# A scan kernel on one core: decays kept in the states' tiles, stores issued an iteration later, one broadcast load in place of two, and an iteration's room for image work by its feed

## The chip, the cores and the metric

The kernel runs on one core of a Trainium2 chip. The metric is the device time in microseconds (us) of one execution; the time before is the median of three runs.

## The reference

The input `x` is [8, 64, 64, 96] in float32: eight images, 64 by 64 positions, 96 channels. Layer 0 adds to it a two-dimensional selective scan:

```
xz = groupnorm(x) @ in_proj_w.T                 # 96 -> 2 x 192, halves xh and z
xc = silu(depthwise 3x3 conv of xh + conv_b)
xs = xc along 4 paths: diagonals, antidiagonals, and both reversed     # 4096 steps each
dt, B, C = x_proj_weight of xs                  # 6, 16 and 16 values per step and path
delta = softplus(dt projected to 192 + bias)
for each of 4096 steps, 192 channels, 16 states n:
    h[n] = h[n] * exp(delta * A[n]) + delta * u * B[n]
    y = sum over n of h[n] * C[n]
y = y + D * xs, the 4 paths put back and added
x = x + (layernorm(y) * silu(z)) @ out_proj_w.T
```

Layer 1 works on each image's 4,096 tokens: a layer norm, six attention heads without softmax, `(q k^T) v`, which the kernel takes in the other order, so that a small Gram matrix per image is enough, then a layer norm and a two-layer perceptron whose factors are rounded to an 8-bit float. Both are added to the tokens.

## The kernel before

**The scan loop.** All work is held together by one loop in `run`. A *step* `m` is an image, a direction `q` (forward or backward) and a chunk of T = 512 of the 4,096 path positions: 8 x 2 x 8 = 128 steps. Both paths of a direction are done together: 2 paths x 64 channels fill 128 partitions, and G = 3 groups of 64 channels make 192. A step has 16 *iterations*, one for each state `n`, so the loop has 2,048 iterations `i = 16 m + n`. The recording order is the order of each engine's instructions: the file schedules by hand, and each engine executes its own queue in order. The framework adds the semaphore waits.

One iteration works on several states at once:

- `decay(i + 2)` on ACT (L966): three exponentials of 128 x 512, the factors `exp(delta * A[n])`, into a `decay` tile, of which there are three.
- `times_b(i + 2)`: the fed value `delta * u * B[n]`, turned, into a `feedT` tile. Who does it is read from `FEED = "DADADAGADADAAAAA"`, a letter for each state: A is ACT (L988, eight instructions of 128 x 192), G is GpSimd (L979), and for D nothing is done here.
- `recur(i)` on VectorE: three scans (L1009), one for each group, from the decays and the PSUM tiles `feed0` to `feed2` into an `h` tile, of which there are six. For a D state VectorE first makes the feed itself, by three multiplications in PSUM (L1013).
- For each part 0, 1 and 2 on TensorE: `turn(i + 1, part)`, which puts the next state's feed of that group into PSUM (four transposes, L996, or for a D state one product with `pick`, L998, in part 0), and then `reduce(i - 4, part)`, four transposes of an older `h` that add up the 16 states in PSUM (L1044).
- `keep(i - 1)` and `read(i - 1)` on GpSimd: the carry for the next chunk (L1025) and `h * C[n]` over 128 x 1536 in place (L1030).
- `fetch(i + 4)`: C[n] of the step as a row of 512 values, broadcast from DRAM (`crow`) to 64 partitions for each of the two paths, into a `cc` tile of [128, 512], of which there are five. It is two loads on SP's queue (L957), one for each path.

After state 15 `place` copies the summed `y` out of PSUM; the forward direction stores it (`part`, L1072), the backward one adds both and stores it, spread to the image (`spread`, L1080 and L1089).

**The images' work.** What comes before and after the scans for each image runs beside the loop, in pieces: `prologue(m)` (the projections of step m, with `crow`'s store at L910 and `delta`), `front` (norm, convolution, `gate`, and `walk`, which reads the image along its diagonals by loads `ut`, L587), and `tail` (`join` and `layers`, with stores of `mid`, `turned` and `out`). These are generators. Each says by a `yield` which engine it needs next and for about how long: `act(us)`, `dve(us)`, `gp(us)`, `pe(us)`, `bank(us)` (TensorE with a PSUM bank). The class `Work` resumes them at fixed places of an iteration, `work.at(tag, place)`: "A" between `decay` and `times_b`, "V" before the third scan, "P" after each part, "G" after `read`, and "S" at the start of an iteration. Each place has a credit: it grows by a gain for each visit, up to a most, and work is resumed while it is positive. `PLACES` holds gain and most. `LAGS` says how many iterations a piece waits after its last engine.

DMA is issued by SP (`nc.sync`) alone, in order: when an issue waits for a semaphore, all that follow wait.

Of the kernel before, what the change touches and what calls it, by code (L numbers as in the profile page):

```python
# [9 lines left out]
F32 = mybir.dt.float32  # L10
# [3 lines left out]
ALU = mybir.AluOpType  # L14
# [21 lines left out]
G = 3  # L36
# [218 lines left out]
    return "P", us, lag, "long" if long else "short"  # L255


SPIN = ("P", 0.0, -1, False)


class Work:
# [1 line left out]

    PLACES = {"A": (2.0, 2.5), "V": (1.5, 2.0), "G": (3.5, 5.0), "P": (0.85, 1.2), "S": (9.0, 9.0)}

    def __init__(self, banks):
        self.now = 0
# [44 lines left out]

        self.long = [x for x in self.long if x is not b]

    def at(self, tag, place=0):
        gain, most = self.PLACES[tag]
        self.credit[tag] = min(most, self.credit[tag] + gain)
        for j in self.urgent + ([] if self.hurried else self.jobs):  # L320
            while not j.done and j.tag == tag:
                if j.ready > (self.now, place) and (j.spin or not self.alone):
                    break
                if not self.alone:
                    if self.credit[tag] <= (0.0 if j not in self.urgent else -1.5 if tag == "P" else -99.0):
# [40 lines left out]
    def finish(self, enough):  # L366

        self.alone = True
        while not enough():
            self.next()  # L370
            for tag, place in (("A", 0), ("V", 0), ("P", 2), ("G", 0)):
                self.at(tag, place)
        self.alone = False
        self.credit = dict.fromkeys(self.PLACES, 0.0)

    def hurry(self, enough):

        self.alone = self.hurried = True
        while not enough():
            self.now += 1  # L380
            for tag, place in (("A", 0), ("V", 0), ("P", 2), ("G", 0)):
                self.at(tag, place)
        self.alone = self.hurried = False

# [89 lines left out]
def front(tc, work, x, k, at, b):  # L474
# [8 lines left out]
    with tc.tile_pool(name=f"f1_{b}", bufs=1, **area) as p1, tc.tile_pool(name=f"f2_{b}", bufs=2, **area) as p2:  # L483
# [33 lines left out]
        def convolve(c):  # L517
# [40 lines left out]
            nc.scalar.activation(pre[:, 0 : len(tiles), :], pre[:, 0 : len(tiles), :], AF.Silu)  # L558
            nc.scalar.activation(z, z, AF.Silu)
            k.tables()  # L560
            nc.sync.dma_start(out=at.gate[:, :, c * CH : (c + 1) * CH], in_=z)

            image = at.image[0 : HH * DOUBLE].rearrange("(h a x c) -> h x a c", a=2, c=DI, x=WW)
# [12 lines left out]
    with tc.tile_pool(name=f"f3_{b}", bufs=3, **area) as p2:  # L576

        def walk(c):
            ut = p2.tile([P, TB, G, 2, GC], F32, tag="ut", name="ut")
            for d in range(2):  # L580
                stride = (2 * WW + 1) * DI if d == 0 else (2 * WW - 1) * DI
                for v in range(2):
                    first = (c * (T // HH) + v + d * WW) * DI
                    rows = at.image[first : first + HH * stride].rearrange("(h x) -> h x", x=stride)
                    rows = rows[:, 0 : TB * 2 * DI].rearrange("h (k x) -> h k x", k=TB)[:, :, 0:DI]
                    for g in range(G):
                        nc.sync.dma_start(  # L587
                            out=ut[v * HH : (v + 1) * HH, :, g, d, :], in_=rows[:, :, g * GC : (g + 1) * GC]
                        )
            u = p2.tile([P, G, T], F32, tag="us", name="us")  # L590
            for g in range(G):
                ps = yield bank(0.45, 4 if g == 0 else 0)
                for i in range(TB):
                    nc.tensor.transpose(ps[:, i * P : (i + 1) * P], ut[:, i, g].rearrange("p d i -> p (d i)"), k.ident)
                yield act(0.6)
                nc.scalar.copy(u[:, g, :], ps)
                work.release(ps)
            for d in range(2):
                nc.sync.dma_start(
                    out=at.seq[d][:, c * T : (c + 1) * T].rearrange("(g i) t -> i g t", i=GC),  # L600
                    in_=u[d * GC : (d + 1) * GC],
                )
            at.walked.add(c)

        yield [walk(c) for c in range(NST)], 3


def tail(tc, work, x, out, k, at, b, last=False):
# [4 lines left out]
    with tc.tile_pool(name=f"t1_{b}", bufs=1, **area) as p1:  # L613
# [5 lines left out]
        with tc.tile_pool(name=f"t2_{b}", bufs=8 if last else 2, **area) as p2:  # L619
# [3 lines left out]
            def join(c):  # L623
# [61 lines left out]
                        )  # L685
                yield act(0.5)
                nc.scalar.copy(t, po)
                if not last:
                    nc.sync.dma_start(out=at.mid[:, s, :], in_=t)
                work.release(ps)  # L690
                yield dve(1.7)
                for i in range(4):
# [32 lines left out]
                if last:  # L725
                    kept[c] = t, xaT
                else:
                    nc.sync.dma_start(out=at.turned[:, c * CH : (c + 1) * CH], in_=xaT)
                joined.add(c)

# [31 lines left out]
        with tc.tile_pool(name=f"t3_{b}", bufs=8 if last else 3, **area) as p2:  # L762

            def layers(c):
# [66 lines left out]
                yield gp(2.0)  # L831
                nc.gpsimd.tensor_tensor(y16, y16, k.b2q, ALU.add)
                nc.gpsimd.tensor_tensor(t, t, y16, ALU.add)
                nc.sync.dma_start(out=out[b].rearrange("(t p) c -> p t c", p=P)[:, s, :], in_=t)

            yield [layers(c) for c in range(NCH)], 8 if last else 3
# [2 lines left out]
def run(tc, psum, dram, x, out, w, NB):  # L839
# [31 lines left out]
            )  # L871
        return images[b]

    made, decays, feeds, hs, carry, sums, other = {}, {}, {}, {}, {}, {}, {}
# [4 lines left out]
    def prologue(m):  # L879
# [26 lines left out]
        x = o.x = tile("x", [NX, T])  # L906
        nc.scalar.activation(x, v, AF.Identity, bias=w.xb)  # L907
        work.release(ps)
        o.crow = dram.tile([2 * NS, T], F32, tag="crow", name=f"crow_{m}", bufs=3)
        nc.sync.dma_start(out=o.crow, in_=x[XC:NX, :])  # L910


        delta = tile("delta", [P, G, T])
        for g in range(G):
            ps = yield bank(0.85)
            nc.tensor.matmul(ps, w.ws[:, q, g, :], x[0 : 2 * NR + 1, :], start=True, stop=True)  # L916
            yield dve(0.6)
            nc.vector.tensor_copy(delta[:, g, :], ps)  # L918
            work.release(ps)
# [32 lines left out]
    def fetch(i):  # L952

        m, n = divmod(i, NS)
        cc = made[m].c[n] = pool.tile([P, T], F32, tag="cc", name=f"cc_{i}", bufs=5)
        for d in range(2):
            nc.sync.dma_start(  # L957
                out=cc[d * GC : (d + 1) * GC], in_=made[m].crow[d * NS + n : d * NS + n + 1, :].to_broadcast([GC, T])
            )

    def decay(i):
        m, n = divmod(i, NS)
        _, q, _ = steps[m]
        decays[i] = pool.tile([P, G, T], F32, tag="decay", name=f"decay_{i}", bufs=3)
        for g in range(G):
            nc.scalar.activation(decays[i][:, g, :], made[m].delta[:, g, :], AF.Exp, scale=w.a_neg[:, q, g, n : n + 1])  # L966

    def times_b(i):

# [30 lines left out]
    def recur(i):  # L1000
        m, n = divmod(i, NS)
        _, q, _ = steps[m]
        h = hs[i] = pool.tile([P, G, T], F32, tag="h", name=f"h_{i}", bufs=6)
        a = decays.pop(i)
        back = slice(None, None, -1) if q else slice(None)

        def scan(g):
            init = carry[m - 1][:, n, g : g + 1] if m % NST else 0.0
            nc.vector.tensor_tensor_scan(h[:, g, back], a[:, g, back], feed[g][:, back], init, ALU.mult, ALU.add)  # L1009

        if FEED[n] == "D":
            for g in (1, 2, 0):
                nc.vector.tensor_tensor(feed[g], feed[0], made[m].du[:, g, :], ALU.mult)  # L1013
# [44 lines left out]
    def place(m):  # L1058
# [7 lines left out]
        for d in range(2):  # L1066
# [1 line left out]
                rows[:, d].rearrange("p k (g i) -> p k g i", i=GC),  # L1068
                y.rearrange("p (k g) (d i) -> p d k g i", g=G, d=2)[:, d],
            )  # L1070
        if q == 0:
            nc.sync.dma_start(out=image(b).part[:, c, :], in_=ys)  # L1072
        else:
            work.start(spread(m, rows), urgent=True)

    def spread(m, rows):
        b, q, c = steps[m]
        for d in range(2):
            yield gp(1.8, 1)
            nc.gpsimd.tensor_tensor(  # L1080
                rows[:, d], rows[:, d], other[m].rearrange("p (d k c) -> p d k c", d=2, k=TB)[:, d], ALU.add
            )
            stride = (3 * WW + 1) * DI if d == 0 else (3 * WW - 1) * DI
            for v in range(2):
                for again in range(2):
# [56 lines left out]
        work.now += tag == "A"  # L1142
        work.at(tag, at)

    LAG = 4
    for i in range(4):
        fetch(i)
    for i in range(2):
        decay(i)
        times_b(i)  # L1150
    for g in range(G):
# [3 lines left out]
    for i in range(total + LAG + 1):  # L1155
# [124 lines left out]
```

## Time and profile before

| | |
|---|---|
| median of 3 runs | 11,243.42 us (11,231.5 to 11,244.23) |
| the profiled execution | 11,245.66 us, of it 11,243.9 us span |
| mean granted TensorE clock | 0.907 |
| scan loop, first scan to last | 244 to 10,996 us |
| busy: TensorE, VectorE, ACT, GpSimd | 81%, 84%, 84%, 83% of the span |
| HBM traffic | 875 MB read, 320 MB written, 106 GB/s |

The profile's span runs from the first instruction to the last of one execution. A group of instructions is a line of the program with its operation and tiles; for it the profile gives busy time, mean duration, and the idle time of the engine just before, with what ended it. Engines are PE (TensorE's products), PEld (its weight loads), DVE (VectorE), ACT, POOL (GpSimd) and SP, whose queue entries are written SPq. A view of waits has, for each pair of waiter and releaser, microseconds in total, times and the longest. A view of windows has, for each stretch, its length, each engine's busy time with its number of instructions, then the TensorE clock, the share of the 16 DMA engines that was busy, and GB/s.

### The profile page before, as it was taken

How to read it: one execution, taken by the hardware profiler on the slowest of the kernel's cores; microseconds unless marked ns; L12 is line 12 of the kernel's file. 1: busy time of each engine (PE TensorE's matmuls, PEld its weight loads, DVE VectorE, ACT ScalarE, POOL GpSimd, SP SyncE). 2: the span in 40 equal slices, each digit the busy share in tenths (PEclk: the TensorE clock that was granted, in tenths of full speed). 3: DMA queues.
4: the chain of work that ended last, by engine and by line, in shares of the span. 5: the costliest groups of instructions: out<-in, count | busy, mean ns of one | idle time of the engine just before them, and what ended most of it. 6: DMA issues, size and time to landing. Idle time of an engine off the chain costs nothing.

```text
span 11243.9 us, 182845 instructions
## 1 busy us (share of the span) xinstructions
PE 9140.0 (81%) x60885; PEld 7661.4 (68%) x60885; DVE 9396.9 (84%) x10582; ACT 9455.9 (84%) x19651; POOL 9365.4 (83%) x7047
## 2 busy tenths in 40 slices
PE   6888788878888788878888788887888878878884
PEld 5677677666676667766677666776667666666663
DVE  2988988888888888888888888888898888989993
ACT  3888888888888888888888888888898888888883
POOL 1877987899878998789987899779997799998994
PEclk8999999888998889988999898998999988889886
DMA  3335333543335443354334543345433543432332
GB/s 91 106 92 143 100 98 92 144 118 102 97 93 149 110 108 95 96 144 113 102 92 113 138 107 102 92 118 134 109 99 90 133 119 104 108 103 84 99 94 63
DMA packets 1122742, 1206.98 MB, mean 107 GB/s; under 512 B 452790, under 2 KB 730007, under 8 KB 1121799
## 3 DMA queue, kind: packets, MB, share of 16 engines
q1 hardware_dynamic: 1121798, 1195.28, 40.3%
q8 instruction: 485, 7.95, 0.3%
q14 instruction: 459, 3.75, 0.1%
HBM read 874.83 MB, written 319.98 MB: 106 GB/s over the span
## 4 chain that ended last, share of the span: by engine, by line
PE 24%; ACT 23%; DVE 17%; POOL 14%; issue 10%; DMA 7%; SPq 4%; DVEq 0%; POOLq 0%; ACTq 0%
DVE h L1009 11%; ACT feedT L988 9%; POOL h L1030 8%; ACT decay L966 7%; PE y L1044 7%; PE feed L996 7%; DMA cc<-crow 4%; DVE feed L1013 4%; PE bank L542 3%; SPq L587 2%; PE bank L894 2%; PE feed L998 1%; ACT L63 1%; POOL du L928 1%; DMA y<-wide 1%
## 5 line engine op out<-in xcount | busy, mean ns | idle before, releaser
L1030 POOL TENSOR_TENSOR h<-h,cc 128x1536 f32<-128x1536 f32 x2048 | 7079.9, 3457 | 458.3 <-DMA cc<-crow 228.9
L1009 DVE TENSOR_TENSOR_SCAN h<-decay,carry,feed 128x512 f32<-128x512 f32 x5376 | 6514.2, 1262 | 810.2 <-PE feed L996 704.8
L966 ACT ACTIVATE decay<-delta,a_neg 128x512 f32<-128x512 f32 x6144 | 3975.0, 714 | 1116.4 <-DVE h L1009 1114.4
L996 PE MATMUL feed<-ident,feedT 128*128 128x128 f32 x16896 | 3090.8, 303 | 1649.1 <-DVE h L1009 1084.6
L1044 PE MATMUL y<-ident,h 128*128 128x128 f32 x24576 | 3847.4, 290 | 130.7 <-POOL h L1030 47.4
L996 PEld LDWEIGHTS feed<-ident,feedT 128*128 128x128 f32 x16896 | 2209.1, 155 | 2246.9 <-ACT feedT L988 840.8
L988 ACT ACTIVATE feedT<-duT,rows 128x192 f32<-128x192 f32 x10240 | 3673.7, 445 | 17.6 <-PE feed L996 14.7
L1044 PEld LDWEIGHTS y<-ident,h 128*128 128x128 f32 x24576 | 3164.5, 152 | 525.2 <-issue 410.3
L1013 DVE TENSOR_TENSOR feed<-feed,du 128x512 f32<-128x512 f32 x1920 | 1200.4, 685 | 162.2 <-PE feed L998 146.5
L1025 POOL COPY carry<-h 128x3 f32<-128x3 f32 x2048 | 402.5, 197 | 877.0 <-DVE h L1009 803.2
L1009 DVE TENSOR_TENSOR_SCAN h<-decay,feed 128x512 f32<-128x512 f32 x768 | 879.5, 1201 | 118.9 <-PE feed L996 106.8
L542 PE MATMUL bank<-wf,xp 97*128 97x192 f32 x4266 | 851.9, 332 | 0.0
L998 PE MATMUL feed<-x,pick 77*128 77x512 f32 x1280 | 708.8, 636 | 3.9
L542 PEld LDWEIGHTS bank<-wf,xp 97*128 97x128 f32 x4266 | 692.8, 194 | 5.4 <-issue 4.6
L928 POOL TENSOR_TENSOR du<-delta,u 128x1536 f32<-128x1536 f32 x128 | 448.4, 3503 | 188.8 <-ACT delta L921 188.8
L916 PE MATMUL bank<-x,ws 13*128 13x512 f32 x764 | 435.5, 650 | 5.6 <-ACT x L907 5.6
L979 POOL TENSOR_TENSOR feedT<-duT,rows 128x512 f32<-128x512 f32 x384 | 396.2, 1060 | 4.7 <-PE feed L996 4.7
L894 PE MATMUL bank<-wx,u 128*128 128x77 f32 x3048 | 360.0, 275 | 0.0
L894 PEld LDWEIGHTS bank<-wx,u 128*128 128x128 f32 x3048 | 352.3, 193 | 1.9 <-ACT duT L936 0.2
L918 DVE COPY delta<-bank 128x512 f32<-128x512 f32 x382 | 256.7, 672 | 86.5 <-PE bank L916 86.1
L934 PE MATMUL bank<-ident,du 128*128 128x128 f32 x1532 | 251.8, 291 | 65.1 <-POOL du L928 61.8
L998 PEld LDWEIGHTS feed<-x,pick 77*128 77x128 f32 x1280 | 211.5, 200 | 97.6 <-DVE h L1009 44.8
(261 smaller groups left out, 6957.4 us busy)
## 6 DMA issues: line engine op xcount, KB each, us to landing
cc<-crow SPq DMA_DIRECT2D x4096, 128.0 KB
u<-seq SPq DMA_DIRECT2D x256, 384.0 KB
wide<-ys SPq DMA_DIRECT2D x512, 192.0 KB
ut<-image SPq DMA_DIRECT2D x768, 64.0 KB
seq<-us SPq DMA_DIRECT2D x128, 384.0 KB
part<-ys SPq DMA_DIRECT2D x64, 768.0 KB
y<-part SPq DMA_DIRECT2D x64, 768.0 KB
y<-wide SPq DMA_DIRECT2D x256, 192.0 KB
```

What stands on the lines that cost most here:

```text
L542: nc.tensor.matmul(v[:, j, :], flat[:, o : o + P], k.wf[:, i, :], start=(i == 0), stop=(i == 8), skip_group_check=True)
L894: nc.tensor.matmul(v[:, j, :], u[:, g, j * P : (j + 1) * P], w.wx[:, q, g, :], start=(g == 0), stop=(g == G - 1))
L916: nc.tensor.matmul(ps, w.ws[:, q, g, :], x[0 : 2 * NR + 1, :], start=True, stop=True)
L928: nc.gpsimd.tensor_tensor(du, delta, u, ALU.mult)
L966: nc.scalar.activation(decays[i][:, g, :], made[m].delta[:, g, :], AF.Exp, scale=w.a_neg[:, q, g, n : n + 1])
L988: nc.scalar.activation(f[part], o.duT[part], AF.Copy, scale=o.rows[:, j, XB + d * NS + n : XB + d * NS + n + 1])
L996: nc.tensor.transpose(feed[g][:, j * P : (j + 1) * P], feeds[i][:, j * G + g, :], w.ident)
L998: nc.tensor.matmul(feed[0], w.pick[:, FEED[:n].count("D"), :], made[m].x, start=True, stop=True)
L1009: nc.vector.tensor_tensor_scan(h[:, g, back], a[:, g, back], feed[g][:, back], init, ALU.mult, ALU.add)
L1013: nc.vector.tensor_tensor(feed[g], feed[0], made[m].du[:, g, :], ALU.mult)
L1030: nc.gpsimd.tensor_tensor(hs[i], hs[i], c.unsqueeze(1).to_broadcast([P, G, T]), ALU.mult)
L1044: nc.tensor.matmul(y[:, j, :], hs[i][:, g, r * P : (r + 1) * P], w.ident, is_transpose=True, start=(n == 0 and j % 4 == 0), stop=(n == NS ...
```

## The change

1. `fetch` loads both paths' rows by one transfer. The source is written as two rows of `crow`, each repeated 64 times, the destination is the whole `cc` tile.
2. The separate `decay` tiles are gone. `decay(i)` writes into the state's own `h` tile, and the scan replaces the decays there. `h` has eight tiles for six, `feedT` three for two. Decays and feeds are made three iterations ahead (`AHEAD`) where it was two.
3. A new yield, `LATER`, stands before the stores of `gate`, `image`, `seq`, `mid`, `turned`, `out`, `crow`, `part` and `wide`: the store is recorded at the start of the next iteration. The store of `mid` moves from before the statistics to beside that of `turned`.
4. The gain of a place depends on the feed. ACT: 1.4 in an iteration that makes an A feed, else 3.0 (2.0 before). VectorE: 0.8 for a D state, else 1.8 (1.5 before). TensorE, for each of three parts: 1.1 for a D state, else 0.74 (0.85 before). The mosts of ACT and VectorE become 3.0 and 2.2.

```diff
+LATER = ("S", 0.0, 1, False)
 SPIN = ("P", 0.0, -1, False)
...
-    PLACES = {"A": (2.0, 2.5), "V": (1.5, 2.0), "G": (3.5, 5.0), "P": (0.85, 1.2), "S": (9.0, 9.0)}
+    PLACES = {"A": (2.0, 3.0), "V": (1.5, 2.2), "G": (3.5, 5.0), "P": (0.85, 1.2), "S": (9.0, 9.0)}
...
-    def at(self, tag, place=0):
-        gain, most = self.PLACES[tag]
+    def at(self, tag, place=0, gain=None):
+        usual, most = self.PLACES[tag]
+        gain = gain or usual
         self.credit[tag] = min(most, self.credit[tag] + gain)
...
         work.release(ps)
+        yield LATER
         o.crow = dram.tile([2 * NS, T], F32, tag="crow", name=f"crow_{m}", bufs=3)
         nc.sync.dma_start(out=o.crow, in_=x[XC:NX, :])
...
-            ps = yield bank(0.85)
+            ps = yield bank(0.85, None if g else 0)
...
         cc = made[m].c[n] = pool.tile([P, T], F32, tag="cc", name=f"cc_{i}", bufs=5)
-        for d in range(2):
-            nc.sync.dma_start(
-                out=cc[d * GC : (d + 1) * GC], in_=made[m].crow[d * NS + n : d * NS + n + 1, :].to_broadcast([GC, T])
-            )
+        nc.sync.dma_start(
+            out=cc, in_=made[m].crow.rearrange("(d n) t -> d n t", n=NS)[:, n : n + 1, :].to_broadcast([2, GC, T])
+        )
...
-        decays[i] = pool.tile([P, G, T], F32, tag="decay", name=f"decay_{i}", bufs=3)
+        hs[i] = pool.tile([P, G, T], F32, tag="h", name=f"h_{i}", bufs=8)
         for g in range(G):
-            nc.scalar.activation(decays[i][:, g, :], made[m].delta[:, g, :], AF.Exp, scale=w.a_neg[:, q, g, n : n + 1])
+            nc.scalar.activation(hs[i][:, g, :], made[m].delta[:, g, :], AF.Exp, scale=w.a_neg[:, q, g, n : n + 1])
...
-        f = feeds[i] = pool.tile([P, TB * G, P], F32, tag="feedT", name=f"feedT_{i}", bufs=2)
+        f = feeds[i] = pool.tile([P, TB * G, P], F32, tag="feedT", name=f"feedT_{i}", bufs=3)
...
-            nc.vector.tensor_tensor_scan(h[:, g, back], a[:, g, back], feed[g][:, back], init, ALU.mult, ALU.add)
+            nc.vector.tensor_tensor_scan(h[:, g, back], h[:, g, back], feed[g][:, back], init, ALU.mult, ALU.add)
...
-        work.at("V")
+        work.at("V", 0, 0.8 if FEED[n] == "D" else 1.8)
         scan(2)
...
-        if q == 0:
-            nc.sync.dma_start(out=image(b).part[:, c, :], in_=ys)
-        else:
-            work.start(spread(m, rows), urgent=True)
+        work.start(spread(m, rows) if q else first_rows(m, ys), urgent=True)
+
+    def first_rows(m, ys):
+        b, _, c = steps[m]
+        yield LATER
+        nc.sync.dma_start(out=image(b).part[:, c, :], in_=ys)
...
-        if i + 2 < total:
-            decay(i + 2)
-        work.at("A")
-        if i + 2 < total:
-            times_b(i + 2)
+        if i + AHEAD < total:
+            decay(i + AHEAD)
+
+        work.at("A", 0, 1.4 if FEED[(i + AHEAD) % NS] == "A" else 3.0)
+        if i + AHEAD < total:
+            times_b(i + AHEAD)
...
-            work.at("P", part)
+            work.at("P", part, 1.1 if FEED[n] == "D" else 0.74)
```

More of the change, by code (lines that the diff above doesn't have):

```diff
@@ L370, in finish @@
             self.next()
-            for tag, place in (("A", 0), ("V", 0), ("P", 2), ("G", 0)):
+            for tag, place in (("A", 0), ("V", 0), ("P", 2), ("G", 0), ("S", 0)):
                 self.at(tag, place)
@@ L380, in hurry @@
             self.now += 1
-            for tag, place in (("A", 0), ("V", 0), ("P", 2), ("G", 0)):
+            for tag, place in (("S", 0), ("A", 0), ("V", 0), ("P", 2), ("G", 0)):
                 self.at(tag, place)
@@ L687, in join @@
                 nc.scalar.copy(t, po)
-                if not last:
-                    nc.sync.dma_start(out=at.mid[:, s, :], in_=t)
                 work.release(ps)
@@ L727, in join @@
                 else:
+                    yield LATER
+                    nc.sync.dma_start(out=at.mid[:, s, :], in_=t)
                     nc.sync.dma_start(out=at.turned[:, c * CH : (c + 1) * CH], in_=xaT)
@@ L833, in layers @@
                 nc.gpsimd.tensor_tensor(t, t, y16, ALU.add)
+                yield LATER
                 nc.sync.dma_start(out=out[b].rearrange("(t p) c -> p t c", p=P)[:, s, :], in_=t)
@@ L872, in image @@
         return images[b]
-    made, decays, feeds, hs, carry, sums, other = {}, {}, {}, {}, {}, {}, {}
+    made, feeds, hs, carry, sums, other = {}, {}, {}, {}, {}, {}
     feed = [psum.tile([P, T], F32, tag=f"feed{g}", name=f"feed{g}") for g in range(G)]
@@ L908, in prologue @@
         work.release(ps)
+        yield LATER
         o.crow = dram.tile([2 * NS, T], F32, tag="crow", name=f"crow_{m}", bufs=3)
@@ L1002, in recur @@
         _, q, _ = steps[m]
-        h = hs[i] = pool.tile([P, G, T], F32, tag="h", name=f"h_{i}", bufs=6)
-        a = decays.pop(i)
+        h = hs[i]
         back = slice(None, None, -1) if q else slice(None)
@@ L1070, in place @@
             )
-        if q == 0:
-            nc.sync.dma_start(out=image(b).part[:, c, :], in_=ys)
-        else:
-            work.start(spread(m, rows), urgent=True)
+        work.start(spread(m, rows) if q else first_rows(m, ys), urgent=True)
+    def first_rows(m, ys):
+        b, _, c = steps[m]
+        yield LATER
+        nc.sync.dma_start(out=image(b).part[:, c, :], in_=ys)
     def spread(m, rows):
@@ L1082, in spread @@
             )
+            yield LATER
             stride = (3 * WW + 1) * DI if d == 0 else (3 * WW - 1) * DI
@@ L1143, in run @@
         work.at(tag, at)
-    LAG = 4
+    AHEAD, LAG = 3, 4
     for i in range(4):
         fetch(i)
-    for i in range(2):
+    for i in range(AHEAD):
         decay(i)
```

## The prediction

> **What bounds the kernel now.** First the page: span, busy shares, DMA, chain.
>
> ```profile
> span 11243.9 us, 182845 instructions
> PE 9140.0 (81%) x60885; PEld 7661.4 (68%) x60885; DVE 9396.9 (84%) x10582; ACT 9455.9 (84%) x19651; POOL 9365.4 (83%) x7047
> q1 hardware_dynamic: 1121798, 1195.28, 40.3%
> PE 24%; ACT 23%; DVE 17%; POOL 14%; issue 10%; DMA 7%; SPq 4%; DVEq 0%; POOLq 0%; ACTq 0%
> cc<-crow SPq DMA_DIRECT2D x4096, 128.0 KB
> ```
>
> No engine is full: four stand at 81 to 84%, and the chain passes through all of them. DMA looks far from a bound (40% of 16 engines). The last line is the largest traffic: 4,096 transfers of 128 KB, 537 MB of 1,195. The loop runs from the first scan at 244 us to the last at 10,996 us: 10,752 us for 2,048 iterations, 5.25 us each; 492 us lie outside it. Windows by 16-state step (step 0, 3, 10, 12 and 14 of one image) show that different engines lead, and that a step is 5 to 10% longer than its fullest engine is busy:
>
> ```profile
> core 0: us, PE busy (x) PEld busy (x) DVE busy (x) ACT busy (x) POOL busy (x), PEclk, DMA share, GB/s
> 4248.50:4323.60 75.10, 59.80 (x397) 50.51 (x396) 67.40 (x67) 66.64 (x141) 71.23 (x45) 0.89 0.38 98
> 4498.20:4588.40 90.20, 79.12 (x544) 67.42 (x543) 73.35 (x74) 76.27 (x149) 64.51 (x36) 1.00 0.31 91
> 5100.60:5190.40 89.80, 72.49 (x490) 61.91 (x489) 75.49 (x103) 74.08 (x163) 83.50 (x91) 0.89 0.47 121
> 5274.50:5349.30 74.80, 61.59 (x421) 52.17 (x419) 68.37 (x67) 64.93 (x139) 69.75 (x41) 0.91 0.39 102
> 5440.60:5528.10 87.50, 70.06 (x492) 56.99 (x491) 81.34 (x96) 78.01 (x167) 79.16 (x75) 0.94 0.40 102
> ```
>
> So only slack between engines is to be won. The waits (us in total, times, longest) say where it sits:
>
> ```profile
> ACT decay L966 <- DVE h L1009: 1114.4, 556, 7.3
> PE feed L996 <- DVE h L1009: 1084.6, 747, 8.1
> DVE h L1009 <- PE feed L996: 811.6, 729, 4.4
> PE feed L996 <- ACT feedT L988: 435.1, 757, 4.5
> POOL h L1030 <- DMA cc<-crow: 228.9, 34, 18.7
> ...
> DVE feed L1013 <- PE feed L998: 146.5, 150, 13.3
> ```
>
> ACT waits for decay tiles to come free, PE and DVE wait for each other, and POOL waits seldom for cc.
>
> Last, one view for how a transfer spreads. At 2,594 us SP issues loads of `turned` (97 rows of 2 KB). The windows around:
>
> ```profile
> 2590.00:2592.00 2.00, 2.00 (x13) 1.28 (x12) 2.00 (x3) 2.00 (x6) 2.00 (x1) 1.00 1.05 219
> 2598.00:2601.00 3.00, 3.00 (x22) 3.00 (x21) 3.00 (x4) 3.00 (x8) 2.92 (x3) 0.72 0.07 26
> ```
>
> The first is transfers of 64 rows: all 16 DMA engines busy, 219 GB/s. The second is one 97-row load alone: a share of 0.07, one engine in sixteen, at 26 GB/s. The trace's packet records there run one after the other, 84 ns per 2,048 B, so 97 rows take 8.1 us. SP is held too: issuing the load of `mid` (L776, median 646 ns) takes 6.11 and 7.43 us behind it.
>
> **The change part by part.**
>
> *One cc load in place of two (L957).* Removed: 2,048 issues on SP at 588 ns (median of L957), 1,204 us of SP's time. Bytes stay. But the shape differs. Before, each load reads 64 repeats of a row into 64 partitions; now the source is written as 2 rows, each repeated 64 times, and the destination as 128 partitions. The row that bears on it is the 97-row load: 97 has no common factor with 16, and one engine did it all. The Trainium skill (DMA: Bandwidth & Descriptors, "Why a DMA increments its semaphore by 16 and not by 1") gives the rule: the number of engines is the largest up to 16 that divides the slowest dimension of both access patterns, and on the SP queue it is the lowest-numbered ones. It makes 1 of 97, as the trace shows, 16 of the old load (64 and 64), and **2 of the new one** (2 and 128). The same page's "Rules for kernel authors" speaks both ways: one 128-partition transfer rather than two halves, and a leading dimension under 16 confines the DMA. No transfer of the trace has unlike leading dimensions that would tell; I take the rule.
>
> By the rule each cc load puts 64 packets on each of two engines: 64 x 84 ns = 5.38 us, against 8 packets, 0.67 us, before. Per iteration that already exceeds 5.25 us. Over the program: 2,048 x 5.38 = 11,010 us. The same lowest engine also has
> - its sixteenth of all other traffic. Now an engine is busy 40.3% of 11,243.9 = 4,531 us; cc's 262,144 packets at 119 ns (mean of the 2 KB packets) are 1,950 us of that, leaving 2,580. With fewer engines busy packets take their usual uncontended times (84 ns at 2 KB, 48 at 768 B, 18 at 256 B, by the packet records), which makes it 2,150;
> - the single-engine transfers: 112 of 97 rows (56 stores and 56 loads of `turned`), 112 x 97 x 84 ns = 913 us less the sixteenth already counted, 856.
>
> Sum: 11,010 + 2,150 + 856 = 14,016 us of work for one DMA engine in the loop. cc is 5 deep, so POOL, waiting for cc at L1030, frees the next buffer as it goes and the engine always has a load queued; Queued behind L1030 on POOL are the next carry, `du` and the images' work; PE's transposes of h (L1044) wait for it, the turns behind them, then DVE and ACT: all keep the queue's pace. What the engine loses is at walks (36 loads of `ut` issued in 24.6 us on SP, during which it gets little), 8 x 25 = 200 us at most. Then 14,016 + 492 outside + 190 = **14,700 us**, against the profiled execution's 11,245.7 (its span 11,243.9 and 1.8 around; 0.02% above the median of 11,243.42). From both sides: the single-engine transfers on another engine and no idle, 11,010 + 2,150 + 492 = 13,650; packets at 90 ns and others at the contended 2,580, 11,796 + 2,580 + 856 + 492 + 200 = 15,900. The mean of 119 ns is left out: it is met with all 16 engines busy, not two. If 16 engines still carry it, the load costs what it did and SP gains.
>
> *The remaining parts* lie under that queue, and I cost them at nothing in the forecast; if the cover is gone they count as follows.
> - LATER: nine kinds of store are issued an iteration later. SP is in order, so cc stood behind SP's waits (399 us for `ys`, 353 for `z`, 231 for `x`). Of POOL's 253 us waiting on cc (L1030 229, L1025 24), seven waits of 16.5 to 18.7 us stand at walks, behind the 36 loads, and stay; some 130 us can go. The price: `crow`, and so `delta`, an iteration later, of 16 ahead.
> - Decays in the states' tiles, three ahead: ACT no longer waits for the scans of i-1 but for PE's last transposes of i-5, issued in iteration i-1 behind the turns. It starts 1 to 2 us later and has one iteration (5.25 us) more. Queued behind that wait are the jobs and feedT; PE waits for these in L996. PE's 540 us waiting for ACT (435 + 105 by the releaser "decay") shrink, but followed back, only about 130 of DVE's 1,347 us of loop idle lie under ACT's work; the rest under PE's own turns and jobs. Nothing in scan (1,262 ns) or exp (714 ns) changes: count and shapes are the same. I take half of 130 + 130.
> - Room by feed: averages stay (ACT 2.0 us an iteration, VectorE 1.49 for 1.5, TensorE 2.56 for 2.55). The third case bounds it at 67 us, and as a gain I give it no more; I take 0.
>
> **The rivals.**
>
> *All 16 engines carry the new load* (7 in 100 faster, 2 in 100 no change). For it: both DRAM and SBUF sides have 128 rows of 2 KB, and only the one reading of the rule splits them by 2. Then 11,246 - 130 = 11,115 us, or, if LATER's gain is taken up by the engine-to-engine waits, about 11,243. Against it: the 97-row load went to one engine although it has 97 packets to spread, so rows are dealt by division and not one by one.
>
> *Sixteen engines, and TensorE's room falls in the wrong iteration* (4 in 100). Where DVE multiplies first (L1013), PE cannot turn until 3 x 685 + 1,262 ns have passed, and the next state's pick (L998) stands behind that iteration's jobs. Room there grows from 2.55 to 3.3 us and shrinks to 2.22 elsewhere: a pair goes from 5.1 to 5.52 us. In steps 1 to 4, where PE is busy 79.12 of 90.20 us, 0.42 x 5 pairs x 32 steps = 67 us. It decides once PE reaches the pick later than DVE ends its scans, which the 146.5 us of L1013 show to happen; 11,310 us.
>
> *Two engines* (87 in 100): 14,700 us. Against it: the rule is seen here on like dimensions alone.
>
> **How the numbers follow.** The likeliest case gives 14,700. Its own bounds, 13,650 to 15,900, drawn in to 13,600 to 15,800, hold some 92 in 100 of it: 0.87 x 0.92 = 0.80, so the range need not reach 11,115. Slower by over 0.2% (22 us, about what a measurement of this kernel can tell from no change): 0.87 + 0.04 = 0.91; within it 0.02; faster 0.07.
>
> **What would show it.** If right: one issue of cc per iteration, 2,048; POOL L1030 waiting on `cc<-crow` over 3,500 us, more than 1,000 times; every engine's busy time nearly as now and its share 62 to 66%; steps of about 105 to 120 us whatever their work, with the lightest (step 0 and 12) grown most; DMA share in a quiet window near 0.13 and near 55 GB/s, and the chain mostly on cc or on SP's issue of it. If cc issues stay at 0.6 us, POOL's wait for cc is under 150 us and DMA stays near 100 GB/s, the rule did not apply and the first two rivals are left: ACT's wait falling tells the first, L1013's wait for L998 growing the other. A time under 13,000 that is above 11,400 would say that packets of two engines overlap and 84 ns is too long.

## The result, and the profile after

The changed kernel takes 14,648.5 us (median of four, 14,647.0 to 14,653.4) against 11,243.8 us before: a ratio of 1.303, interval 1.3008 to 1.3053. The profiled execution's span is 14,651.6 us. From its page, the span, the busy times, the DMA queue, the group of `h * C` on POOL and the issues of cc:

```profile
span 14651.6 us, 179085 instructions
PE 9771.6 (67%) x60885; PEld 8238.9 (56%) x60885; DVE 9437.5 (64%) x10582; ACT 9500.7 (65%) x19651; POOL 9300.8 (63%) x7047
q1 hardware_dynamic: 1060358, 1195.04, 27.7%
L1035 POOL TENSOR_TENSOR h<-h,cc 128x1536 f32<-128x1536 f32 x2048 | 7059.2, 3447 | 4816.0 <-DMA cc<-crow 4317.4
cc<-crow SPq DMA_DIRECT2D x2048, 256.0 KB
```

The group of `h * C` before:

```profile
L1030 POOL TENSOR_TENSOR h<-h,cc 128x1536 f32<-128x1536 f32 x2048 | 7079.9, 3457 | 458.3 <-DMA cc<-crow 228.9
```

VectorE, ACT and POOL are busy for as long as before, within 0.7%; TensorE is busy 7% longer for the same number of instructions. POOL's time for one `h * C` is the same, 3,447 ns for 3,457; it is the idle time before it that went from 458 to 4,816 us, and 4,317 us of that ended with a cc load. The DMA engines look *less* busy than before, 27.7% of sixteen for 40.3%.

The third line holds the cause in a count. The queue carried 1,121,798 packets before and 1,060,358 now, 61,440 fewer. By the trace's packet records these are all of 4 bytes, 120,523 before and 59,083 now, and there are as many packets of 2 KB as there were (375,408). The count fits one 4-byte packet from each engine that takes part in a transfer: 4,096 loads on 16 engines make 65,536, 2,048 loads on 2 engines make 4,096, and the difference is 61,440 exactly.

A quiet window, in which only cc flows, and SP's timeline there:

```profile
core 0: us, PE busy (x) PEld busy (x) DVE busy (x) ACT busy (x) POOL busy (x), PEclk, DMA share, GB/s
8198.00:8208.00 10.00, 7.81 (x37) 7.82 (x38) 0.70 (x1) 6.69 (x14) 5.83 (x3) 0.57 0.13 50
```

```profile
8190.98 21.45 SPq L962 DMA_DIRECT2D cc<-crow  x4
```

A share of 0.13 is two engines of sixteen, at 50 GB/s, twice the 26 of the single 97-row load. SP is no longer free either: four issues of cc take 21.45 us, 5.36 us each, where one took 0.59. That is the 64 x 84 ns = 5.38 us of the prediction, as if SP were held until the two engines had room for the next load. The waits say what it does to the rest (us in total, times, longest):

```profile
POOL h L1035 <- DMA cc<-crow: 4317.4, 1247, 27.6
DVE h L1014 <- PE feed L1002: 2764.6, 1017, 32.2
...
ACT h L972 <- PE y L1049: 1162.1, 387, 13.7
...
PE bank L597 <- DMA ut<-image: 579.2, 46, 25.0
...
PE y L1049 <- POOL h L1035: 438.2, 222, 7.3
```

POOL waits for cc (first line), TensorE's transposes of h wait for POOL (last line), the turns stand behind those, and then VectorE and ACT wait for PE (second and third line). Loads that have nothing to do with cc are late as well: those of the walks (`ut`) now hold TensorE up for 579 us; before, 29. The page's chain breaks off early here: its shares add up to 10% of the span. The kernel `merged_only` below, which differs from the kernel before by this load alone, has a whole one.

The windows by step, for steps 0, 3, 10, 12 and 14 of the same image as before, and step 5 last:

```profile
5512.20:5607.80 95.60, 61.92 (x384) 51.40 (x383) 66.36 (x66) 66.09 (x140) 73.22 (x44) 0.82 0.29 82
5810.50:5916.90 106.40, 83.50 (x542) 72.10 (x542) 73.75 (x74) 76.49 (x149) 63.73 (x36) 0.89 0.24 76
6620.50:6741.10 120.60, 78.40 (x485) 65.94 (x484) 75.36 (x102) 76.09 (x167) 86.14 (x93) 0.80 0.32 91
6857.70:6962.70 105.00, 67.10 (x416) 55.46 (x414) 68.87 (x67) 65.62 (x140) 65.75 (x39) 0.79 0.25 75
7085.60:7203.30 117.70, 80.33 (x492) 65.26 (x491) 82.15 (x96) 78.33 (x165) 81.19 (x77) 0.77 0.26 77
6023.00:6150.50 127.50, 70.79 (x447) 60.04 (x446) 70.74 (x70) 75.65 (x154) 62.02 (x37) 0.76 0.27 79
```

Step 5 before, which the prediction did not show:

```profile
4679.30:4759.20 79.90, 68.44 (x453) 56.74 (x451) 70.59 (x70) 70.59 (x143) 51.79 (x30) 0.94 0.37 94
```

None of these six steps is under 16 x 5.38 = 86 us, whatever its engines do; the fullest engine, busy for 69 to 86 us, leaves a fifth to two fifths of each step unused.

### The profile page after: what moved, and what is told of

Its sections match the earlier page's. It is cut to its first block, busy times and chain, and to the rows that moved or that the text cites. A ratio compares the mean times of both kernels' runs of the same rounds, so it can differ in the third digit from the quotient of the medians.

```text
span 14651.6 us, 179085 instructions
## 1 busy us (share of the span) xinstructions
PE 9771.6 (67%) x60885; PEld 8238.9 (56%) x60885; DVE 9437.5 (64%) x10582; ACT 9500.7 (65%) x19651; POOL 9300.8 (63%) x7047
## 2 busy tenths in 40 slices
DMA packets 1061273, 1206.49 MB, mean 82 GB/s; under 512 B 391349, under 2 KB 668566, under 8 KB 1060358
## 3 DMA queue, kind: packets, MB, share of 16 engines
q1 hardware_dynamic: 1060358, 1195.04, 27.7%
## 5 line engine op out<-in xcount | busy, mean ns | idle before, releaser
L1035 POOL TENSOR_TENSOR h<-h,cc 128x1536 f32<-128x1536 f32 x2048 | 7059.2, 3447 | 4816.0 <-DMA cc<-crow 4317.4
L1014 DVE TENSOR_TENSOR_SCAN h<-h,carry,feed 128x512 f32<-128x512 f32 x5376 | 6549.8, 1264 | 2590.3 <-PE feed L1002 2453.4
L972 ACT ACTIVATE h<-delta,a_neg 128x512 f32<-128x512 f32 x6144 | 3973.4, 712 | 3079.6 <-issue 1563.0
L1049 PE MATMUL y<-ident,h 128*128 128x128 f32 x24576 | 4089.9, 303 | 449.0 <-POOL h L1035 438.2
L1049 PEld LDWEIGHTS y<-ident,h 128*128 128x128 f32 x24576 | 3369.5, 160 | 924.5 <-POOL h L1035 552.9
L1002 PEld LDWEIGHTS feed<-ident,feedT 128*128 128x128 f32 x16896 | 2341.6, 163 | 1829.7 <-DVE h L1014 1008.9
L1014 DVE TENSOR_TENSOR_SCAN h<-h,feed 128x512 f32<-128x512 f32 x768 | 884.8, 1203 | 333.3 <-PE feed L1002 311.2
L940 PEld LDWEIGHTS bank<-ident,du 128*128 128x128 f32 x1532 | 212.8, 167 | 984.9 <-POOL du L934 957.1
L942 ACT COPY duT<-bank 128x512 f32<-128x512 f32 x383 | 218.3, 570 | 617.0 <-PE bank L940 617.0
L597 PE MATMUL bank<-ident,ut 128*128 128x128 f32 x748 | 143.2, 330 | 586.7 <-DMA ut<-image 579.2
L1072 ACT COPY ys<-y 128x768 f32<-128x768 f32 x256 | 192.1, 802 | 480.6 <-PE y L1049 480.5
```

Of the source, the lines that this page charges most:

```text
L940: nc.tensor.transpose(ps[:, i * P : (i + 1) * P], du[:, g, r * P : (r + 1) * P], w.ident)
L972: nc.scalar.activation(hs[i][:, g, :], made[m].delta[:, g, :], AF.Exp, scale=w.a_neg[:, q, g, n : n + 1])
L1002: nc.tensor.transpose(feed[g][:, j * P : (j + 1) * P], feeds[i][:, j * G + g, :], w.ident)
L1014: nc.vector.tensor_tensor_scan(h[:, g, back], h[:, g, back], feed[g][:, back], init, ALU.mult, ALU.add)
L1035: nc.gpsimd.tensor_tensor(hs[i], hs[i], c.unsqueeze(1).to_broadcast([P, G, T]), ALU.mult)
L1049: nc.tensor.matmul(y[:, j, :], hs[i][:, g, r * P : (r + 1) * P], w.ident, is_transpose=True, start=(n == 0 and j % 4 == 0), stop=(n == NS ...
```

## The experiments

Each time stands as a ratio to runs of the kernel before on the same chip, since their medians moved between 11,242 and 11,258 us. Two kernels are called different where the 95% intervals of their ratios do not meet.

### The cause: five kernels

**`two_loads`** puts the two loads back and leaves all else of the change:

```diff
-        nc.sync.dma_start(
-            out=cc, in_=made[m].crow.rearrange("(d n) t -> d n t", n=NS)[:, n : n + 1, :].to_broadcast([2, GC, T])
-        )
+        for d in range(2):
+            nc.sync.dma_start(
+                out=cc[d * GC : (d + 1) * GC], in_=made[m].crow[d * NS + n : d * NS + n + 1, :].to_broadcast([GC, T])
+            )
```

> The changed kernel with the two cc loads of 64 rows each back in fetch; all else of the change stays. Theory (the new load is dealt to two DMA engines only): the whole loss goes, about 11,115 us, between 10,980 and 11,330 with what the other parts do; POOL waits for cc under 200 us and the packet count of the queue is back at 1.122 million. Rival (the tiles, the lead of three and the later stores cost most of the 3,405 us): above 12,500 us.

11,157.8 us, ratio 0.9922 (0.9909 to 0.9934). The queue line is that of before to the packet:

```profile
q1 hardware_dynamic: 1121798, 1195.28, 40.1%
```

The theory held. The whole loss lies in this edit, and the rest of the change gains 0.8%.

**`merged_only`** is the converse: the kernel before, with those lines the other way round.

> The kernel before with nothing changed but the cc load: one transfer of [2, 64 repeats] into 128 partitions. Theory: 14,600 to 14,900 us, since one DMA engine's 14,016 us of loop work are the same and the other parts lie under it; the packet count falls by 4,096 x 16 - 2,048 x 2 = 61,440. Rival (other parts share in the loss): under 13,500 us.

14,649.0 us, ratio 1.3026 (1.3006 to 1.3046), the same as the whole change. Its packet count is that of the changed kernel:

```profile
q1 hardware_dynamic: 1060358, 1195.04, 27.8%
```

The chain that ended last, followed back over the whole span, stands on this load more than on anything else; in the kernel before cc was 4% of it:

```profile
DMA cc<-crow 38%; POOL h L1029 10%; PE feed L995 3%; DMA u<-seq 3%; DVE h L1008 3%; PE y L1043 3%; ACT feedT L987 3%; ACT decay L965 2%; DMA gate<-z 2%; DMA image<-pre 2%; POOL du L928 1%; SPq L956 1%; PE bank L542 1%; SPq L1088 1%; SPq L776 1%
```

The other parts, worth 0.8% without the merged load, are worth nothing beside it: here, slack won between the other engines had no price while the DMA engines set the pace.

**`lead16`** keeps one load into 128 partitions and changes what its source leads with. The C rows stand eight times in DRAM:

```diff
-        o.crow = dram.tile([2 * NS, T], F32, tag="crow", name=f"crow_{m}", bufs=3)
-        nc.sync.dma_start(out=o.crow, in_=x[XC:NX, :])
+        o.crow = dram.tile([2, 8, NS, T], F32, tag="crow", name=f"crow_{m}", bufs=3)
+        for d in range(2):
+            nc.sync.dma_start(
+                out=o.crow[d].rearrange("r n t -> n r t"),
+                in_=x[XC + d * NS : XC + (d + 1) * NS, :].unsqueeze(1).to_broadcast([NS, 8, T]),
+            )
...
-            out=cc, in_=made[m].crow.rearrange("(d n) t -> d n t", n=NS)[:, n : n + 1, :].to_broadcast([2, GC, T])
+        rows = made[m].crow.rearrange("d r n t -> (d r) n t")[:, n : n + 1, :]
+        nc.sync.dma_start(out=cc, in_=rows.to_broadcast([16, 8, T]))
```

> The changed kernel, still one cc load into 128 partitions, but the step's C rows stand eight times in DRAM, so that the load's source leads with 16 rows, each repeated 8 times; the store of crow is eight times as large, in two transfers. Theory: 16 engines again, 8 packets on each, and the loss goes with one load kept: 11,050 to 11,300 us, within 0.5% of the kernel with two loads, SP's issues of cc 2,048. Rival (one large transfer is the trouble, whatever its leading dimension): stays above 14,000 us.

11,165.5 us, ratio 0.9926 (0.9914 to 0.9939), no different from two loads. The issue of cc on SP (its line of source; shortest, median and longest in ns):

```profile
L967 SPq DMA_DIRECT2D cc<-crow x2048: 514/521/2359, 227.9 to 10897.1; - x187
```

One 256 KB load is issued in 521 ns, and 2,048 of them in 1.07 ms, for the two loads' 2.4 ms. So neither the size of the transfer nor the merge was the trouble but the 2 that the source led with. (The larger store of `crow` costs nothing that shows.) That SP has 1.3 ms less to do is worth nothing here.

**`lead4`** is the same with two copies of each row, so that the source leads with 4.

> As the kernel with one load led by 16 rows, but the C rows stand twice, so the load leads with 4 rows, each repeated 32 times: four engines, 32 packets on each, 2.69 us an iteration. Theory (it is one engine's sum against the loop): 2,048 x 2.69 = 5,505 us and 3,006 us of other work on the lowest engine, 8,511 us, under the loop's 10,670; so hidden, 11,120 to 11,260 us, the upper end if cc's landing four times as late reaches POOL. Rival (time goes with the number of engines lost): well above, 11,700 us or more.

11,334.8 us, ratio 1.0082 (1.0069 to 1.0095): above the theory's range and far under the rival's. Its packets say that four engines took part:

```profile
q1 hardware_dynamic: 1070598, 1203.45, 37.5%
```

That is 51,200 fewer than with two loads: 65,536 - 2,048 x 4 = 57,344 fewer packets of 4 bytes for cc, and 128 x 48 = 6,144 more for the larger store of `crow` (32 of data and 16 of 4 bytes a step). The engine's sum, 8,511 us, is under the loop as the theory has it, and 95% of the loss is gone, but 1.6%, some 180 us, over two loads are left. POOL's waits for cc, first in `lead4`, then in `two_loads`:

```profile
POOL h L1038 <- DMA cc<-crow: 451.0, 71, 22.9
```

```profile
POOL h L1036 <- DMA cc<-crow: 174.8, 24, 20.1
```

They fall in bursts: followed by step, 316 of the 451 us lie in steps 5 to 7, where the walks' loads, 36 at a time, stand ahead of cc on SP (96 us there with two loads), and 69 in steps 12 and 13 (58). So a mean under the pace was not enough. The likely reason is that cc has to catch up after such a block, and at an estimated 2.69 us a load (32 x 84 ns) it does so four times as slowly as at 0.67; no run tried this apart.

**`split97`** keeps the load on two engines and relieves the lowest of another traffic: each 97-row store and load of `turned` is cut.

```diff
-                    nc.sync.dma_start(out=xaT, in_=at.turned[:, c * CH : (c + 1) * CH])
+                    for rows in (slice(0, DM), slice(DM, DM + 1)):
+                        nc.sync.dma_start(out=xaT[rows], in_=at.turned[rows, c * CH : (c + 1) * CH])
...
-                    nc.sync.dma_start(out=at.turned[:, c * CH : (c + 1) * CH], in_=xaT)
+                    for rows in (slice(0, DM), slice(DM, DM + 1)):
+                        nc.sync.dma_start(out=at.turned[rows, c * CH : (c + 1) * CH], in_=xaT[rows])
```

> The changed kernel with its one cc load as it is, but each store and load of turned, 97 rows, cut into 96 rows and 1 row. Theory (single-engine transfers ran on the same lowest engine as half of each cc load): that engine's work falls by 112 x 97 x 84 ns = 913 us less 112 x 7 x 84 ns = 66 us, about 850 us, so 13,800 us. Rival (they ran on another engine, or beside): within 150 us of 14,650.

13,961.9 us, ratio 1.2414 (1.2397 to 1.2431): 687 us less than the changed kernel, far outside the rival's 150. So the 97-row transfers did run on an engine that carries cc; 163 us of the 850 do not come back. The changed kernel's own trace shows the place too. At 3,343.71 us SP issues a load of `turned` while cc loads are still under way:

```profile
3344.00:3352.00 8.00, 8.00 (x52) 8.00 (x52) 3.46 (x3) 1.80 (x3) 3.58 (x2) 0.68 0.14 52
3358.00:3364.00 6.00, 0.00 (x0) 0.00 (x0) 2.23 (x2) 0.12 (x1) 3.55 (x2) 0.61 0.06 25
```

At first two engines are busy (a share of 0.14) and no third beside them, so the load stands behind cc; later one engine works alone (0.06, 25 GB/s) and cc's other engine has nothing to do.

### The other parts, without the merged load: seven kernels

**`usual_room`** is `two_loads` with the room as before:

```diff
-    PLACES = {"A": (2.0, 3.0), "V": (1.5, 2.2), "G": (3.5, 5.0), "P": (0.85, 1.2), "S": (9.0, 9.0)}
+    PLACES = {"A": (2.0, 2.5), "V": (1.5, 2.0), "G": (3.5, 5.0), "P": (0.85, 1.2), "S": (9.0, 9.0)}
-        work.at("A", 0, 1.4 if FEED[(i + AHEAD) % NS] == "A" else 3.0)
+        work.at("A")
...
-        work.at("V", 0, 0.8 if FEED[n] == "D" else 1.8)
+        work.at("V")
...
-            work.at("P", part, 1.1 if FEED[n] == "D" else 0.74)
+            work.at("P", part)
```

> The changed kernel with two cc loads and the room as before (ACT 2.0 of at most 2.5, VectorE 1.5 of at most 2.0, TensorE 0.85 in every iteration). Theory (the room does nothing, the gain of 92 us is from later stores and lead): within 25 us of 11,158. First rival (the room is what pays): 11,210 to 11,250. Second rival (the room is set against the feeds, as TensorE's in the multiplied iterations): 11,090 to 11,130.

11,182.9 us, ratio 0.9948 (0.9935 to 0.9961): the new room is worth 0.26% here, with intervals that only just do not meet. That is some 29 us, just past the 25 that the theory allowed.

**`no_later`** is `two_loads` with each store recorded where it was before (and the first bank of `delta`, which goes with it, asked for as before). Two of the seven places:

```diff
-            yield LATER
             nc.sync.dma_start(out=at.gate[:, :, c * CH : (c + 1) * CH], in_=z)
...
-        work.start(spread(m, rows) if q else first_rows(m, ys), urgent=True)
+        if q == 0:
+            nc.sync.dma_start(out=image(b).part[:, c, :], in_=ys)
+        else:
+            work.start(spread(m, rows), urgent=True)
```

> The changed kernel with two cc loads and every store recorded where it was, without LATER. Theory (SP's waits for stores held cc, some 130 us of POOL's waiting, half of it real): 11,200 to 11,260 us, and POOL waits for cc 230 us or more, against 175 with later stores. Rival (the lead of three alone makes the gain): within 25 us of 11,158.

11,290.7 us, ratio 1.0048 (1.0035 to 1.0061). Slower than the kernel before, and by more than the theory allows. POOL's wait for cc is 257 us, 82 more than in `two_loads`; SP waits 485 us for `z` where it was 82, and 456 for `ys` where it was 53:

```profile
POOL h L1032 <- DMA cc<-crow: 257.0, 35, 21.1
```

```profile
SPq L563 <- ACT z L561: 485.1, 64, 10.2
SPq L1074 <- ACT ys L1069: 455.7, 57, 16.9
```

**`ahead2`** is `two_loads` with separate decay tiles, the numbers of tiles of before and the lead of two. These go together in all that follows; "the lead" stands for the three, and no run parts them:

```diff
-    AHEAD, LAG = 3, 4
+    AHEAD, LAG = 2, 4
-        hs[i] = pool.tile([P, G, T], F32, tag="h", name=f"h_{i}", bufs=8)
+        decays[i] = pool.tile([P, G, T], F32, tag="decay", name=f"decay_{i}", bufs=3)
...
-        h = hs[i]
+        h = hs[i] = pool.tile([P, G, T], F32, tag="h", name=f"h_{i}", bufs=6)
+        a = decays.pop(i)
```

> The changed kernel with two cc loads, and decays in tiles of their own again, made two iterations ahead (decay 3, h 6, feedT 2 tiles); later stores and the new room stay. Without later stores the kernel with the lead of three took 11,291 us, 49 above the kernel before, and the room gave 25, so the theory is that decays in the states' tiles cost some 75 us (ACT waits for PE's last transposes): about 11,085 us. Rival (the longer lead pays as forecast, half of 130 us): 11,200 to 11,240.

11,251.8 us, ratio 1.0010 (1.0004 to 1.0017). The theory fell: with later stores and the new room it is the lead that pays, 0.9%. That is the rival's direction, but more than it said.

**`later_only`** is the kernel before with the later stores, that is, the edits of `ahead2` and `usual_room` together. One of the seven places against the kernel before:

```diff
             k.tables()
+            yield LATER
             nc.sync.dma_start(out=at.gate[:, :, c * CH : (c + 1) * CH], in_=z)
```

> The kernel before with the later stores alone: two cc loads, tiles, lead and room as before. Theory: later stores are worth the 133 us that they were with the lead of three: 11,110 us (11,090 to 11,135). Rival (they mend what the lead does, since ACT then waits for PE and SP for ACT): 11,200 to 11,240.

11,226.3 us, ratio 0.9987 (0.9980 to 0.9993). The theory of 133 us fell too, and the rival's range held; alone, later stores are worth 0.13%.

**`ahead_only`** is the kernel before with decays in the states' tiles and the lead of three, the edits of `no_later` and `usual_room` together. Against the kernel before:

```diff
-    LAG = 4
+    AHEAD, LAG = 3, 4
-        decays[i] = pool.tile([P, G, T], F32, tag="decay", name=f"decay_{i}", bufs=3)
+        hs[i] = pool.tile([P, G, T], F32, tag="h", name=f"h_{i}", bufs=8)
```

> The kernel before with decays in the states' tiles and the lead of three alone: two cc loads, stores where they were, room as before. With later stores the lead took 11,226 to 11,183 us, and without them, with the new room, the kernel stood at 11,291. First theory (the lead needs the later stores, whatever the room): 11,280 to 11,320 us. Rival (without later stores it is the new room that costs, and the lead pays its 43 us): about 11,200 us.

11,199.7 us, ratio 0.9948 (0.9934 to 0.9961). The rival holds. The lead alone is worth 0.52%, and without later stores it was the new room that cost. The six (with `two_loads`) make a table, as ratios to the kernel before, which itself has the lead of two, stores in place and the room as before:

| | room as before | new room |
|---|---|---|
| lead of two, stores later | 0.9987 | 1.0010 |
| lead of three, stores in place | 0.9948 | 1.0048 |
| lead of three, stores later | 0.9948 | 0.9922 |

The new room costs 1.0% where stores are in place, costs 0.2% with the lead of two and later stores, and gains 0.3% with both others. What makes it cost so much without later stores was not tried further. SP's waits for `z` and POOL's for cc are no proof, as `ahead_only` has the one just as long (465 us) and the other longer (312 us) at 0.9948.

What the lead changes can be read at the tiles. First `ahead2`: ACT's wait before it writes decays, and TensorE's two waits for feeds that ACT makes (PEld its weight loads, PE its products). Then the same two kinds of wait in `two_loads`:

```profile
ACT decay L973 <- DVE h L1016: 819.5, 432, 6.9
PEld feed L1003 <- ACT feedT L995: 786.1, 1009, 4.4
...
PE feed L1003 <- ACT feedT L995: 338.7, 794, 3.9
```

```profile
ACT h L973 <- PE y L1050: 370.9, 222, 9.1
...
PEld feed L1003 <- ACT feedT L995: 228.0, 133, 5.0
```

With the lead of three ACT waits for PE's transposes (371 us) where it waited for the scans (820 us), and the weight loads' wait for feeds falls from 786 to 228 us, from 1,009 times to 133.

**`two_split`** and **`ahead2_split`** are `two_loads` and `ahead2` with the 97-row transfers cut as in `split97`.

> The changed kernel with two cc loads and the 97-row transfers cut into 96 and 1 rows. Theory: in the kernel before SP was held 117 us in all by the issues behind these loads (L776), some of it while POOL ran out of cc; at most 50 us come off the 11,158 of two loads: 11,105 to 11,160. Rival (112 more issues of 0.6 us on SP and nothing won): 11,160 to 11,190.

> As the kernel with later stores, the new room, two loads and the lead of two, and the 97-row transfers cut into 96 and 1. Theory: the 30 us that the cut gave with the lead of three add up: about 11,055 us, the fastest here. Rival (the cut's gain and the lead's cost are the same waits): within 15 us of the lead of two without the cut.

`two_split`: 11,127.6 us, ratio 0.9902 (0.9887 to 0.9916), the fastest kernel of the study, 1.0% under the kernel before and 24% under the changed one, and within the theory's range. Against `two_loads` it is 0.2%, and the intervals overlap, so this gain alone is not shown. `ahead2_split`: 11,221.1 us, ratio 0.9981 (0.9974 to 0.9988), clear of `ahead2`'s 1.0010 by 0.3%, 31 us on one chip. So the cut's gain is there without the lead as well, though the 11,055 us expected for `ahead2_split`, which took over the wrong price of the lead, was missed.

## Why the prediction was right, point by point

- **Two engines, the rule of the divisor.** The rule was taken from the Trainium skill (DMA: Bandwidth & Descriptors, "Why a DMA increments its semaphore by 16 and not by 1"), which lets both sides' slowest dimensions bound the number of engines; with 2 and 128 the runs agree. Shown: by the packet count, by the window of 0.13 and 50 GB/s, by `merged_only`, where this edit alone makes the loss, and by `lead16` and `lead4`, where a leading 16 or 4 in place of 2 takes it away. The prediction had only transfers with like leading dimensions to go by.
- **5.38 us a load.** Measured on SP as 5.36; in the quiet window 50 GB/s on two engines make 2,048 B every 82 ns on each, 5.25 us for 64.
- **14,016 us in the loop and 190 of idle.** The loop runs from 247 to 14,376 us, 14,128; the forecast sum was 14,206. Outside stand 523 us for the 492 taken over. The total is 51 us under the forecast. That it came so near is in part luck, by the next point but one.
- **The single-engine transfers on the same engine, 856 us.** `split97` gave 687 for the 850 of its cut. The place was right, the term some 20% too large as a difference. Where the other 163 us went was not tried; an engine that has less to do may stand idle more of the time, which the sum leaves out.
- **Packets of 84 ns, and 2,150 us of other traffic.** For cc the 84 ns held, and the 119 ns of the trace of before was rightly left out. For the other traffic the same step failed: its packets were to take their uncontended times once fewer engines are busy. But 27.7% of 14,651.6 us on 16 engines is 64,936 us; less 2 x 11,010 for cc that leaves 42,916, or 2,682 us an engine, close to the 2,580 of before. (The 768 B packets, by their records, took 52.0 ns in the mean and 51.5 before, not 48.) With 2,682 for 2,150 the sum is 14,548 us, 420 more than the loop took. What hides it is seen in part: cc's packets follow each other every 82 ns, 260 us less over 2,048 loads than at 84, and the packets' records overlap somewhat, since a window of before had a share of 1.05. So two engines and the size of cc's term are shown, and the exact total is partly a cancelling of errors.
- **The other parts at nothing under the queue.** Right, by `merged_only` against the changed kernel. Their own sizes, which counted only for the rival: the lead was put at half of 130 us and gave 58 alone (0.52% of 11,243) and 99 beside later stores and the new room. Later stores were put at 65 us and gave 15 alone, none beside the lead with the old room, and 142 beside the lead with the new room. The step that failed there is POOL's wait for cc as their price: it fell from 229 to 166 us in `later_only`, and a quarter of that at most reached the end. The room was put at 0 and is anything from +1.0% to -0.3%, depending on the two others. The first rival's 11,115 us would have been 11,158.
- **What was to be seen.** POOL waits 4,317 us, 1,247 times, where over 3,500 and 1,000 were said; VectorE, ACT and POOL stand at 63 to 65%, and cc's quiet window at 0.13 and 50 GB/s where 55 was said. TensorE does not fit: it stands at 67%, its busy time up by 632 us. Wrong, too, are the steps: they were to take 105 to 120 us, the lightest growing most, and the six shown take 95.6 to 127.5. Step 5, with the walks' loads, grew more (from about 80 to 127.5 us) than step 0 (75.1 to 95.6). The load on the engine does not spread evenly: what other traffic a step has, and what SP issues ahead of cc, seem still to set its length.
- **Two readings that are off without harm.** Of the steps shown before, step 3 is 14% longer than its fullest engine is busy, not 5 to 10%. And of POOL's waits for cc before, six, not seven, are of 16.5 us and more.

## What to carry to other kernels

Before a transfer is merged or reshaped, look at the first dimension of *both* its sides: here a source of 2 rows, each repeated 64 times, put 256 KB on two DMA engines of sixteen and made them the bound of a kernel whose DMA stood at 40%. The busy share of sixteen engines cannot show this, since it falls; a window's GB/s over the share does, as do a count of packets and the time that the issuing queue is held. Slack between engines, worth 0.8% here, was worth nothing while two DMA engines set the pace, and small schedule edits are to be measured together: here the new room changed its sign with the others.

## What the runs showed of the hardware that had not been expected

- SP is held when the load that it issues goes to two busy DMA engines: an issue of cc took a median of 3,313 ns and at most 8,991, for 521 when sixteen engines carry the same 256 KB. SP issues in order, so all that stands behind it is late as well.
- TensorE's granted clock fell from 0.907 to 0.81 in the changed kernel, and its busy time rose from 9,140 to 9,772 us for the same instructions; with 96 and 1 rows it was 0.827, and in all kernels near 11,200 us 0.897 to 0.913. It was low where TensorE waited most, and no run tells cause from effect. TensorE was busy 67% of the span even so, and the loss goes and comes with the load alone.
- A load that leads with 97 rows runs on one engine, 8.1 us for 194 KB (97 x 84 ns). Cut into 96 and 1 it gave 0.3% in one pair of kernels and, not clear of the noise, 0.2% in another, although the sixteen engines stand at 40% in the mean; POOL's wait for cc fell with it, from 195 to 125 us and from 175 to 144.
